# A two-layer transformer on one core: second-layer q and k projected between the layer norms, with changes to the first loads, a bias product and the tail of the first attention

## Chip, core and metric

The kernel runs on one core of a Trainium2 chip. The metric is the device time of one execution, in microseconds (us). The engines are TensorE (PE, with its weight loads PEld), VectorE (DVE), ScalarE (ACT), GpSimd (POOL) and SyncE (SP), which here only issues DMAs. All data are 32-bit floats. A 128x128 matmul against 512 columns appears in the trace as two records.

## What is computed

Two sequences (B = 2) of T = 2048 tokens with D = 256 features, 16 heads of 16. Each layer is an attention and a gated part that both read the normalized input; the layer's input x gets their product added.

```python
# layer 0, xn = layernorm(x)
attn = softmax(q @ k.T / sqrt(D)) @ v; attn = attn @ w_o.T + b_o + xn
Q, K = xn @ W_Q.T, xn @ W_K.T
out = branch(Q, K, V_fwd, W_fwd, U_fwd) + alpha * branch(Q @ W_inv.T, K @ W_inv.T, ...)
#   branch: (Q.V) * cumsum(K.W) per expert, weighted by softmax of a gelu router, times U, plus weights @ b
x = x + attn * silu(out @ W_O.T)
# layer 1, xn = layernorm(x)
attn = softmax(q @ k.T * HD**-0.5 + band mask of +-64) @ v; attn = attn @ w_out + b_out
gate = softmax(xn @ gate_w.T)                     # 8 experts
y = xn @ weight.T + sum_e gate_e/16 * (xn @ lora_U_e.T) @ lora_V_e.T
x = x + attn * silu(y)
```

## The kernel before

Features lie on partitions (two chunks of 128, NC = 2), tokens on columns. x, xn (normalized input) and gt (the gate) of both sequences stay in SBUF. Tokens go in blocks of 512 (TB; four blocks n per sequence). A scheduler orders the instructions of each engine ahead of time by their dependences and its own costs; what is marked keep_in_program_order ("pin") stays where the program puts it. Each engine works its list in order, and a wait holds everything behind it.

The stages, with lines:

- Start (L173 to L232). Weights of layer 0 come on ACT's and SP's DMA queues; load_x brings the eight x blocks. product (L204) multiplies weights together ahead of time; layer_norms (L95) runs the first layer's norms between these steps. A norm of one block is `there` (eight 128x128 transposes to tokens on partitions, xt, L104), statistics on DVE (L108, L110), Sqrt on ACT (L113), two small DVE steps, `back` (four scalings on ACT, xc, L121; eight transposes to xb, L127; copies to xn by ACT and DVE, L129).
- Layer 0's gate (L263 to L413): router (L277, L290), then for each block eight chunks of px, py, po (L387, L391, L371). The weights times b is the product of a 16-row bO with a 16-row wT, once for each output half (L403). we and wT come by SP from DRAM.
- attention(A0) (from L416). Projections of q and k (keys_queries, L456) go through DRAM (qd<-sb, L461) so that each head gets 32 rows; values (L469). Then a loop over steps s: 32 items (sequence b, head group g, block n) of U = 16 key tiles each. A step computes the transposed scores sk of item i and, U + 3 steps ahead, the untransposed sq for the row maxima (both L605), exponentials on ACT (L621), the maxima on DVE (L617), and one step later the weighted sum acc (L664). ACT copies acc to SBUF (`more`, L674) and POOL adds it to av (L675). After an item, its division is done by a chain of DMAs on SP (away, compact, invert, write, spread, divide), for the last item by PE and DVE (last_there L725 to L729, last_back L742). project (L750) multiplies by the output weights, DVE multiplies by gt (L755), POOL adds to x (L756). sk, acc, pr and others share one PSUM ring of four banks, tag "m".
- In the last U + 3 = 19 steps there is no sq any more.
- Layer 1's norms (L905 to L923): as before, for all eight blocks, with the router gates (L849), their return to tokens on partitions (tokens, L860), softmax (normalized) and turned (L876), which sends the weights through DRAM to 16 rows per expert (ge).
- Experts (L883): per block pt, po (L887, L893), tg on DVE, a second matmul with lV (L897), Silu, update of x with the attention bias times the gate.
- attention(A1), with the band: keys_queries for sequence 0 (16 jobs, L456), values for sequence 0, then sequence 1's projections while the first scores run.

Weights of an attention live in one pool, wat0 for layer 0, closed after its attention, then wat1.

Of the kernel before, what the change touches and what calls it, by code (L numbers as in the profile page):

```python
# [10 lines left out]
F32 = mybir.dt.float32  # L11
I32 = mybir.dt.int32
AF = mybir.ActivationFunctionType
ALU = mybir.AluOpType
# [23 lines left out]
def two_layers(ctx: ExitStack, tc: tile.TileContext, a, out):  # L38
# [20 lines left out]
    load_x(0, 0)  # L59
# [13 lines left out]
    def load_attn(pool, l, eng):  # L73
        return dict(
            q=load(pool, f"wq{l}", [P, NC, D], rows(a[f"wq{l}"]), eng),
            k=load(pool, f"wk{l}", [P, NC, D], rows(a[f"wk{l}"]), eng),
            v=load(pool, f"wv{l}", [P, NC, D], rows(a[f"wv{l}"]), eng),
            o=load(pool, f"wo{l}", [P, NC, D], rows(a[f"wo{l}"]), eng),
            bq=load(pool, f"bq{l}", [P, NC], a[f"bq{l}"], eng),
            bk=load(pool, f"bk{l}", [P, NC], a[f"bk{l}"], eng),  # L80
            bo=load(pool, f"bo{l}", [P, NC], a[f"bo{l}"], eng),
            bv=load(pool, f"bv{l}", [P, NC], a[f"bv{l}"], eng),
        )
# [10 lines left out]

    def layer_norms(blocks, tmp, ps, between=lambda r: None):  # L95


        QT = TB // P

        def there(b, n):  # L100
            xt = ps.tile([P, QT, D], F32, name="xt", tag="xt")
            for t in range(QT):
                for c in range(NC):
                    nc.tensor.transpose(xt[:, t, bass.ts(c, P)], x[b][:, c, bass.ds(n * TB + t * P, P)], ident)  # L104
            st = tmp.tile([P, QT, 6], F32, name="st", tag="st")
            mv = tmp.tile([P, QT, 2], F32, name="mv", tag="mv")
# [4 lines left out]

            f = tmp.tile([P, 2, QT], F32, name="f", tag="f")
            nc.scalar.activation(f[:, 0, :], mv[:, :, 1], AF.Sqrt, bias=eps_t)  # L113
            nc.vector.reciprocal(f[:, 0, :], f[:, 0, :])
            nc.vector.scalar_tensor_tensor(f[:, 1, :], mv[:, :, 0], -1.0, f[:, 0, :], ALU.mult, ALU.mult)
# [16 lines left out]
        for r in range(len(blocks) + 1):  # L132
            first = there(*blocks[r]) if r < len(blocks) else None
            if held:
                back(*held)
            held = first
            between(r)
# [12 lines left out]
    layer0 = ctx.enter_context(ExitStack())  # L150
    wat0 = layer0.enter_context(tc.tile_pool(name="wat0", bufs=1))

# [6 lines left out]
    with tc.tile_pool(name="fw", bufs=1) as fw:  # L159
# [4 lines left out]
        bO = fw.tile([2 * KE, D], F32, name="bO")  # L164
# [4 lines left out]
        with tc.tile_pool(name="raw", bufs=1) as raw, tc.tile_pool(name="tn", bufs=2) as tn, tc.tile_pool(  # L169
# [3 lines left out]
            wq = load(raw, "wq", [P, NC, D], rows(a["W_Q"]), nc.scalar)  # L173
            wiT = load(raw, "wiT", [P, NC, D], rows(a["W_invT"]), nc.scalar)
            wk = load(raw, "wk", [P, NC, D], rows(a["W_K"]), nc.scalar)
# [14 lines left out]
            bT = load(raw, "bT", [P, NC, 2 * KE], rows(a["bT"]), nc.sync)  # L190
# [32 lines left out]
            product(lambda m: bO, bT, 2 * KE, woT)  # L223
# [10 lines left out]
        A0 = load_attn(wat0, 0, nc.sync)  # L234
# [13 lines left out]
        nc.vector.reciprocal(rn, rn)  # L248
        ones = fw.tile([P, TB], F32, name="ones")
# [13 lines left out]
        with tc.tile_pool(name="pa", bufs=2, space=PSUM) as pa, tc.tile_pool(  # L263
# [87 lines left out]
            with tc.tile_pool(name="ta", bufs=2) as ta:  # L351
                for b in range(B):
                    prev = None
                    for n in range(NB):
# [9 lines left out]
                        wT = ta.tile([2 * KE, TB], F32, name="wT", tag="wT")  # L364
                        nc.sync.dma_start(out=wT, in_=wd[b][:, cols])
# [36 lines left out]
                        for oc in range(NC):  # L402
                            nc.tensor.matmul(po[oc], bO[:, bass.ts(oc, P)], wT, start=False, stop=True)  # L403
# [12 lines left out]
    def attention(A, scale, local, final):  # L416
# [14 lines left out]
        with ExitStack() as st:  # L431
# [20 lines left out]
            def keys_queries(b, n, i, hf, bank, place):  # L452
                w, bias = ((A["k"], A["bk"]), (A["q"], A["bq"]))[i]
                ps = bank()
                for c in range(NC):
                    nc.tensor.matmul(  # L456
# [547 lines left out]
```

## Time and profile before

| | us |
|---|---|
| median of three runs | 2598.02 (2597.92 to 2598.47) |
| the profiled execution | 2595.75, span 2594.0 |
| PE busy | 2543.6 (98% of the span) |
| DVE, ACT, POOL busy | 1681.6, 1633.7, 893.3 |
| first PE matmul | at 8.21 |
| layer 0's gate, per block | 43.3 |
| attention 0's steps with sq, each | 2.93 |
| last scores of attention 0 end | about 2117.0 |
| layer 1's norms | 2132.7 to 2178.4 |
| experts | 2178.4 to 2236.5 |
| q and k of sequence 0, layer 1 | 2236.5 to 2264.2 |
| values of sequence 0, layer 1 | 2264.2 to 2279.7 |

The page gives busy time, and a busy engine need not be the one that sets the end: the chain of waits, followed back from the last instruction, tells which one does. The table's later rows come from the timeline of PE. Stretches (windows) give the busy time of each engine between two times. A time in brackets behind an instruction is how long its engine stood idle ahead of it, and whose signal ended that.

### The profile page before, as it was taken

The numbers are of one execution on the slowest core, as the hardware profiler recorded it, in microseconds if no ns is written. First come the engines' busy times: TensorE is split into PE (matmuls) and PEld (weight loads), VectorE is DVE, ScalarE is ACT, GpSimd is POOL, SyncE is SP. The second block draws the span as 40 slices with busy tenths as digits, with TensorE's granted clock in tenths as the row PEclk, the third lists the DMA queues.
The fourth block names the chain that finished last, engine by engine and source line by source line (L and its number), as shares of the span: only waits on it lengthen the run. The fifth ranks groups of instructions, "written<-read, shape, count | busy, mean of one in ns | idle before, by whom it ended". The sixth has DMA issues, their size and how long they took to land.

```text
span 2594.0 us, 48140 instructions
## 1 busy us (share of the span) xinstructions
PE 2543.6 (98%) x18916; PEld 1075.1 (41%) x18916; DVE 1681.6 (65%) x2755; ACT 1633.7 (63%) x3188; POOL 893.3 (34%) x836
## 2 busy tenths in 40 slices
PE   8999999999999999999999999999999988999998
PEld 5444444543333333333333333333333325467765
DVE  4143333258888888888777888888888714138875
ACT  5400000127888888888878888888888874236654
POOL 0000000102444444444444444444444440107776
PEclk9999999999999999999999999999999999999999
DMA  7031111320001001010000001010000012234542
GB/s 246 37 85 49 50 49 33 121 74 3 16 10 49 12 11 47 12 44 16 10 22 36 12 21 37 12 46 14 10 16 12 10 34 35 73 123 129 157 143 85
DMA packets 80098, 129.83 MB, mean 50 GB/s; under 512 B 27456, under 2 KB 32448, under 8 KB 77056
## 3 DMA queue, kind: packets, MB, share of 16 engines
q1 hardware_dynamic: 77824, 125.19, 15.4%
q8 instruction: 148, 2.42, 0.4%
q10 hardware_dynamic: 2048, 1.58, 0.2%
q14 instruction: 78, 0.64, 0.1%
HBM read 80.23 MB, written 45.97 MB: 49 GB/s over the span
## 4 chain that ended last, share of the span: by engine, by line
PE 93%; DVE 3%; DMA 2%; ACT 1%; issue 1%; POOL 0%; POOLq 0%; ACTq 0%; SPq 0%; DVEq 0%
PE sk L605 24%; PE acc L664 21%; PE sq L605 18%; PE pp L456 4%; PE py L391 4%; PE po L371 4%; PE px L387 4%; PE pr L750 2%; PE ph L277 2%; PE pp L469 2%; PE psf L204 1%; DVE seen L612 1%; PE po L893 1%; DMA q<-row 1%; PE xb L127 1%
## 5 line engine op out<-in xcount | busy, mean ns | idle before, releaser
L617 DVE TENSOR_REDUCE part<-sq 128x2 f32<-128x1024 f32 x1024 | 1206.6, 1221 | 302.2 <-PE sq L605 301.8
L621 ACT ACTIVATE e<-sk 128x512 f32<-128x512 f32 x2048 | 1063.0, 615 | 215.9 <-PE sq L605 194.2
L605 PE MATMUL sk<-q,k 32*128 32x512 f32 (+2 forms) x5632 | 1153.9, 533 | 12.3 <-DMA q<-row 5.5
L605 PE MATMUL sq<-k,q 32*128 32x512 f32 (+2 forms) x5120 | 1131.4, 569 | 1.3 <-DVE part L617 1.3
L675 POOL TENSOR_TENSOR av<-av,more 128x512 f32<-128x512 f32 x480 | 607.9, 1266 | 962.5 <-ACT more L674 962.4
L605 PEld LDWEIGHTS sk<-q,k 32*128 32x128 f32 x5632 | 530.3, 184 | 604.3 <-ACT e L621 491.8
L664 PE MATMUL acc<-e,v 128*32 128x512 f32 x4096 | 550.6, 605 | 0.0
L605 PEld LDWEIGHTS sq<-k,q 32*128 32x128 f32 x5120 | 403.5, 183 | 22.2 <-DVE part L617 12.2
L674 ACT COPY more<-acc 128x512 f32<-128x512 f32 x480 | 287.8, 600 | 2.5 <-PE acc L664 1.5
L664 PEld LDWEIGHTS acc<-e,v 128*32 128x32 f32 x4096 | 82.5, 108 | 391.5 <-ACT e L621 386.2
L407 ACT ACTIVATE gt<-po 128x512 f32<-128x512 f32 x16 | 9.5, 596 | 324.6 <-PE po L403 324.6
L612 DVE CUSTOM_DVE_ANT_0 seen<-sq,mask 128x256 f32<-128x256 f32 (+1 forms) x512 | 176.7, 408 | 48.7 <-PE sq L605 42.6
L413 POOL TENSOR_TENSOR x<-x,up 128x512 f32<-128x512 f32 x16 | 20.2, 1265 | 459.2 <-DVE up L410 459.2
L626 POOL TENSOR_SCALAR_AFFINE_SELECT xn<-xn 128x512 f32<-128x512 f32 x172 | 110.0, 671 | 90.7 <-ACT xn L621 89.6
L395 DVE TENSOR_TENSOR xs<-we,px 128x512 f32<-128x512 f32 x64 | 43.9, 685 | 136.5 <-PE px L387 135.4
L621 ACT ACTIVATE xn<-sk 128x512 f32<-128x512 f32 x172 | 90.7, 601 | 55.5 <-PE sk L605 26.9
L387 PE MATMUL px<-xn,FV 128*128 128x512 f32 x256 | 121.2, 595 | 0.0
L391 PE MATMUL py<-cum,FW 128*128 128x512 f32 x256 | 120.5, 593 | 0.6 <-DVE cum L360 0.6
L371 PE MATMUL po<-pr,UO 128*128 128x512 f32 x256 | 119.0, 592 | 0.0
L397 DVE TENSOR_TENSOR pr<-xs,py 128x512 f32<-128x512 f32 x64 | 44.0, 687 | 61.3 <-PE py L391 61.1
L755 DVE TENSOR_TENSOR upd<-gt,pr 128x512 f32<-128x512 f32 x32 | 22.0, 687 | 81.4 <-PE pr L750 76.3
L371 PEld LDWEIGHTS po<-pr,UO 128*128 128x128 f32 x256 | 48.6, 190 | 61.2 <-issue 60.5
(167 smaller groups left out, 1634.6 us busy)
## 6 DMA issues: line engine op xcount, KB each, us to landing
we<-wd SPq DMA_DIRECT2D x128, 128.0 KB
ad<-av SPq DMA_DIRECT2D x60, 256.0 KB
qd<-sb SPq DMA_DIRECT2D x48, 256.0 KB
k<-qd SPq DMA_DIRECT2D x10, 1024.0 KB
q<-qd SPq DMA_DIRECT2D x10, 1024.0 KB
xn<-ad SPq DMA_DIRECT2D x60, 128.0 KB
recb<-rd SPq DMA_DIRECT2D x60, 128.0 KB
q<-qd SPq DMA_DIRECT2D x12, 512.0 KB
```

What stands on the lines that cost most here:

```text
L371: nc.tensor.matmul(po[oc], UO[:, ch, bass.ts(oc, P)], pr, start=(ch == 0), stop=False)
L387: nc.tensor.matmul(px, FV[:, c, bass.ts(ch, P)], xn[b][:, c, cols], start=(c == 0), stop=(c == NC - 1))
L391: nc.tensor.matmul(py, FW[:, c, bass.ts(ch, P)], cum[:, c, :], start=(c == 0), stop=(c == NC - 1))
L456: nc.tensor.matmul(ps, w[:, c, bass.ts(hf, P)], xn[b][:, c, bass.ts(n, TB)], start=(c == 0), stop=(c == NC - 1))
L605: nc.tensor.matmul(o, lhs, rhs, start=True, stop=True)
L612: nc.vector.tensor_tensor_reduce(seen[:, lo:hi], sq[:, d, t * 2 * P + lo : t * 2 * P + hi], mask[:, lo:hi], 1.0, LOWEST, ALU.add, ALU.max, ...
L617: nc.vector.tensor_reduce(pt[:, pair[0] : pair[1] + 1, t, kb], sq, AX.X, ALU.max)
L621: nc.scalar.activation(e, t, AF.Exp, scale=scale)
L626: nc.gpsimd.affine_select(out=e[:, :, c, :], in_=e[:, :, c, :], compare_op=ALU.is_ge, fill=0.0, base=0, pattern=[[0, 4], [sign, P]], chann ...
L664: nc.tensor.matmul(acc[hp[j], o : o + hi - lo], vs[b][:, kt, vcols(g, j)], es[j][:, lo:hi], start=(r == 0), stop=(r == len(parts) - 1), sk ...
L674: nc.scalar.copy(more, acc)
L675: nc.gpsimd.tensor_tensor(avs[i], avs[i], more, ALU.add)
```

## The change

Seven edits together.

1. The first DMA on SP is wq of layer 0's gate, the first on ACT is its wiT; x(0,0) follows wq on SP.
2. bO and wT are held twice, at rows 0 to 15 and 32 to 47; the second output half takes the upper copy. bT gets 48 columns, wT a second DMA.
3. Both layers' attention weights share one set of buffers (pool wat). wq, wk, and lU with lV (in wv's buffer) of the second layer are loaded at step 0 of attention 0; its biases, gateT and baseT at the start; wo after attention 0; wv after the experts.
4. In the last 19 steps of attention 0 DVE adds acc straight from PSUM to av.
5. In those steps sequence 0's norm begins: its transposes in halves (norm_there), a copy to xn as a resting place and the statistics by DVE; one `factors` for all four blocks at the end. The scalings (norm_apply: two tiles of four on DVE, two on ACT), the transposes back, and gates, tokens and normalized of sequence 0 follow among the last item's division and projection.
6. Sequence 1's norm runs after the attention, and between its steps 12 of the 16 q and k projections of sequence 0; the other four come between the experts of the two sequences. attention(A1) starts with values(0). Their sb ring has three buffers.
7. In experts lV's product comes at once after its own po; ge comes by four DMAs per sequence with the rows in the order of rank, then expert (lU and lV are laid out to match), in place of eight. One PSUM pool serves this stage, with one pt bank and not two. The row buffer of attention 0's maxima is single.

```diff
-    load_x(0, 0)
...
-            wq = load(raw, "wq", [P, NC, D], rows(a["W_Q"]), nc.scalar)
+            wq = load(raw, "wq", [P, NC, D], rows(a["W_Q"]), nc.sync)
             wiT = load(raw, "wiT", [P, NC, D], rows(a["W_invT"]), nc.scalar)
+            load_x(0, 0)
...
-        bO = fw.tile([2 * KE, D], F32, name="bO")
+        bO = fw.tile([HP + 2 * KE, D], F32, name="bO")
+        twice = [slice(r * HP, r * HP + 2 * KE) for r in range(NC)]
...
-                        for oc in range(NC):
-                            nc.tensor.matmul(po[oc], bO[:, bass.ts(oc, P)], wT, start=False, stop=True)
+                        for oc, r in enumerate(twice):
+                            nc.tensor.matmul(po[oc], bO[r, bass.ts(oc, P)], wT[r, :], start=False, stop=True)
...
+    def norm_there(b, n, half, bank, tmp, mv, copy, issue=lambda i: i):
+        H2 = QT // 2
+        xt = bank().rearrange("p (t d) -> p t d", d=D)
...
+        rest = resting(b, n, half)
+        copy(rest, xt)
...
+            nc.vector.bn_stats(st[:, t, :], rest[:, t, :])
+    def norm_apply(b, n, f):
+        for t in range(QT):
+            rest = resting(b, n, t // 2)[:, t % 2, :]
+            if t % 2:
+                nc.scalar.activation(rest, rest, AF.Identity, scale=f[:, 0, t : t + 1], bias=f[:, 1, t : t + 1])
+            else:
+                nc.vector.tensor_scalar(rest, rest, f[:, 0, t : t + 1], f[:, 1, t : t + 1], ALU.mult, ALU.add)
...
+                elif i * U + u >= len(items) * U - U - LEAD and u:
+                    nc.vector.tensor_tensor(avs[i], avs[i], acc, ALU.add)
...
+                for r in range(2 * NB):
+                    n, half = divmod(r, 2)
+                    at(total - U - LEAD + 1 + 2 * r, norm_there, 0, n, half, single, op, mv[:, tile_of(n), :], nc.vector.tensor_copy, pin)
+                at(total - 1, factors, nf, mv, pin)
+                for f, *args in (
+                    (last_there, last),
+                    (norm_apply, 0, 0, nf[:, :, tile_of(0)]),
+                    (last_back, last),
+                    (back, 0),
+                    (norm_apply, 0, 1, nf[:, :, tile_of(1)]),
+                    (project, last, 0),
...
+            there(0)
+            project(2)
+            there(1)
+            factors(nf[:, :, two(0)], mv[:, two(0), :])
+            whole_bias(A1, small())
+            turned(pl, 0)
+            project(2)
+            norm_apply(1, 0, nf[:, :, tile_of(0)])
+            norm_apply(1, 1, nf[:, :, tile_of(1)])
+            there(2)
+            project(1)
+            there(3)
+            factors(nf[:, :, two(1)], mv[:, two(1), :])
+            project(1)
+            norm_back(1, 0, bank)
...
+            project(len(jobs))
+            for n in range(NB):
+                experts(1, n)()
+    A1["v"] = weight(1, "v")
+
+    attention(A1, float(HD ** -0.5), True, True, projected=True)
```

Here project(count) is count of keys_queries for sequence 0 of layer 1.

## The prediction

> **What bounds the kernel now.** I read the page's busy shares and its chain first, then the stages by time, then the groups of instructions and their waits inside the stages that the diff touches. From the page:
>
> ```profile
> PE 2543.6 (98%) x18916; PEld 1075.1 (41%) x18916; DVE 1681.6 (65%) x2755; ACT 1633.7 (63%) x3188; POOL 893.3 (34%) x836
> PE 93%; DVE 3%; DMA 2%; ACT 1%; issue 1%; POOL 0%; POOLq 0%; ACTq 0%; SPq 0%; DVEq 0%
> ```
>
> 93% of the chain is TensorE (PE). Such a kernel is shortened by removing PE work from the chain, or by filling the places where PE waits. The stages between the two attentions show where that is: attention 0's last steps, its drain, the layer norms, the experts, the q/k projection of sequence 0.
>
> ```profile
> 2067.60:2117.00 49.40, 49.40 (x314) 12.79 (x317) 3.43 (x7) 45.13 (x93) 27.70 (x22) 1.00 0.04 12
> 2117.00:2132.70 15.70, 10.85 (x41) 4.39 (x37) 3.04 (x6) 4.95 (x8) 6.42 (x6) 0.89 0.13 36
> 2132.70:2178.40 45.70, 34.84 (x288) 23.31 (x288) 25.18 (x112) 27.92 (x56) 1.27 (x1) 0.85 0.09 25
> 2178.40:2236.50 58.10, 57.15 (x144) 25.39 (x144) 17.89 (x29) 12.93 (x22) 0.46 (x1) 1.00 0.27 38
> 2236.50:2264.20 27.70, 27.67 (x65) 12.09 (x65) 0.75 (x1) 10.30 (x15) 9.42 (x10) 1.00 0.42 126
> ```
>
> Columns: stretch, its length, then busy time of PE, PEld, DVE, ACT, POOL. In rows 2 and 3 (61.4 us) PE stands still for 15.7 us, and what it does is short transposes; the chain of waits there gives 33 us to PE and 30 to DVE, ACT and hand-overs. Row 5 is pure PE, full, needing only block data that exist 60 us earlier. So row 5 can fill rows 2 and 3. Single waits, from PE's timeline:
>
> ```profile
> 8.21 3.75 PE L204 MATMUL psf<-wq,wiT 128*128 128x256 f32 x8 [8.21 <-DMA wiT<-in_W_invT]
> ...
> 258.47 1.98 PE L403 MATMUL po<-wT,bO 16*128 16x512 f32 x4
> 260.38 1.98 PE L387 MATMUL px<-xn,FV 128*128 128x512 f32 x4
> ...
> 2115.80 1.14 PE L605 MATMUL sk<-q,k 32*128 32x512 f32 x8
> ...
> 2123.42 0.66 PE L725 MATMUL tr<-ident,av 128*128 128x128 f32 x4 [2.57 <-POOL av L675]
> ...
> 2138.15 2.70 PE L127 MATMUL xb<-ident,xc 128*128 128x128 f32 x8 [3.50 <-ACT xc L121]
> ```
>
> PE's first matmul waits 8.2 us for a weight. The two bias matmuls of a block (L403) take 260.38 − 258.47 = 1.91 us one after the other, while four score matmuls (L605) with 32 rows each take 1.07 us start to end in the chain.
>
> **What the Trainium skill says.** "TensorEngine Tiling (Array Packing)", Key Properties: row tiles of 32 work in parallel when they lie in different row groups. L605 agrees: four of 512 columns in 1.07 us, where one full-array matmul of 512 columns takes 0.86 (two of L456 in 1.72). "DMA: Bandwidth & Descriptors", Queues, rings and completion order: the engines take turns between queues packet by packet. The first load agrees: below. Same page, Anatomy of one DMA: about 2.0 us fixed plus bytes over 436 GB/s; the chain of waits agrees on the fixed part, with 2.69 us for 8 KB (rd<-dn) and 2.37 for 128 KB (recb<-rd). "TensorE: Matmul & The Clock Gate", Part 1: after idling the array runs at half rate until it has been busy some 3.4 us. L204's first 16 records take 0.47 us each, its last 32 take 0.22.
>
> **The change part by part**, against the profiled execution (2595.75 us, span 2594.0), which is 2.27 below the median 2598.02.
>
> 1. *First transfers.* wq leads SP's queue, wiT leads ACT's, x(0,0) goes behind wq. Now wiT is second on ACT, while SP moves x. Data flow from 2.4 us at 370 GB/s; x rows have 2 KB, weight rows 1 KB, so ACT's queue has a third, 123 GB/s: 0.52 MB in 4.2 us, 6.6 us, and PE starts 1.5 later. After: the two weights come first, 0.52 MB at 370 GB/s is 1.4 us, so 3.8 + 1.5 = 5.3. Gain 2.9, I take 2.7. Next are wk and x(0,0), some 2 us of data later, by 7.5; they are needed at 9.7 and 13.3. No other load is waited for in the first 60 us. Bounds 1.0 and 4.7 (the clock may also rise during the second product). SP gets seven more small loads (some 3 us); its next urgent transfer, wd, is issued at 117 us, the queue is through by 64.
> 2. *Bias pair.* The second copy of bO and wT lies 32 rows higher, so both matmuls run in two row groups: 1.91 becomes 0.86 + 0.15. 8 blocks × 0.9 = 7.3 us, all on PE, which is busy 43.0 of 43.0 us per block there. It costs one more wT DMA per block, 0.31 us on SP, which idles in that stage. The price of a pair is not shown; bounds: 1.91 (nothing gained) and 0.86 (8.4).
> 3. *Attention 0's last 19 steps.* ACT's copies (0.49 of 2.45 us a step) and POOL's adds go; DVE adds from PSUM (0.69), it was idle. ACT then needs 4 × 0.49 = 1.96 a step, PE 2.07. Added on PE: sequence 0's transposes, 32 × 0.11 = 3.5. New PE sum: 19 × 2.07 + 3.5 + 0.2 (pmx) + 4 × 1.91 (L750) = 50.7, now 52.2. DVE gets per two steps 2 × 0.69 + 0.69 + 0.9 = 3.0 of 4.6. The PSUM ring "m" of four now serves the transposes too; each bank is read one step later, so I expect no wait. Gain 1.0; bounds +1.5 and −3.
> 4. *Drain and sequence 0's norms.* After the last scores: L750 1.9, acc 1.0, add 0.75, tr 0.7, DVE's reciprocal and division 1.0, of 1.5, back-transposes 4 × 0.87, L750 2 × 1.72, gates 4 × 0.72, tokens 0.8: 17.4. Evacuations I set at 1.5, the PSUM pools' change 0.7: 19.6.
> 5. *Sequence 1's norms with q and k.* PE: there 3.5, back 3.5, gates 2.9, tokens 0.8, turned 1.8, bias 1.0, twelve projections × 1.72 = 20.6: 34.1, plus 1.0 of waits. The chain norm_there, copy, statistics, factors, apply takes some 6 us twice; between the two ends stand 5 to 6 us of projection. ACT has 25 us of work in it. Each projection brings its SP transfer (256 KB); ge needs 4 broadcasts instead of 8.
> 6. *Experts.* 8 × 6.87 + turned 1.8 + four projections 6.9 = 63.7; the one pt bank is free after 0.7 us, behind 3.4 us of po.
> 7. *A new wait.* The layer's wv shares its buffer with lU and lV, so its load starts after the last expert matmul, and values(0), next on PE, needs it: 0.5 issue + 2.4 + 0.6 data = 3.5. v's memset (4.1 us of 8.26 for two, POOL) now also starts there, but six PSUM banks cover the last us. Behind values(0) on PE stand sequence 1's projections and the first scores, all moved by the wait. On SP the q/k fetches queue behind wv; PE needs them 20 us later. Bounds of the wait: 2.5 and 6.
>
> The other moved loads cost nothing: wq, wk, lU, lV of the second layer are issued on SP at attention 0's step 0, when PE has read the old buffers, and behind them stands q<-row of a block 13 steps (38 us) away; wo follows the last L750, and its first reader, the bias product, comes some 10 us later; gateT and baseT leave ACT's queue, where their issue took 0.4 to 0.5 us each between the last exponentials.
>
> Sum of 4 to 7: 19.6 + 35.1 + 63.7 + 3.5 = 121.9 against rows 2 to 5, 147.2: gain 25.3. All parts: 2.7 + 7.3 + 1.0 + 25.3 = 36.3. 2595.75 − 36.3 = 2559.5; with the 2.27, **2562**. The main loops issue the same instructions in the same order, at no cost.
>
> **The rivals.**
> - *In-order ACT holds PE in part 5.* Applies, copies, sb and gT stand in one queue behind waits on DVE. About twelve hand-overs from DVE, each holding PE 0.8 us, take 10 back: 2572. For it: the norms now have PE waits of 3.5 us; against: q/k stand between.
> - *The pair stays serial.* Both write full columns; then 7.3 is lost: 2569. Against: L605 overlaps in the same form.
> - *Better.* The half clock of the norm stage (0.85 granted) goes, and the start warms earlier: another 7, 2555.
> - *Slower: the ring of three sb.* A projection waits until the DMA of the third before has landed, and ACT, holding, keeps norms and PE waiting. With landing time L, twelve jobs take 4 × (L + 0.7); it eats 36 us from 4(L + 0.7) = 71, L = 17 us. At L = 20 the time is 2609. Against: before, sixteen such jobs ran at 1.72 us each on a ring of four without one wait, so L is below 6.2.
> - *Nothing changes:* only if parts 4 to 7 give back all; no view supports that.
>
> **How the numbers follow.** Likeliest case 0.53 (2555 to 2569), ACT 0.20, pair 0.10, better 0.10, none 0.02, slower 0.05. The range, 2551 to 2576, takes the first four with their bounds and leaves the upper tail of the ACT case out. A measurement here tells some 0.2%, 5 us, from no change. Faster 0.93, same 0.02, slower 0.05.
>
> **What would show it.** PE's first matmul near 5.3 us; the bias group's start-to-next at 1.0 us; steps of 2.1 to 2.5 us before the drain; values starting some 36 us earlier than 2264.2, after one PE wait of 3 to 4 us for wv; no PE wait over 1.5 us between. PE waits for ACT above 8 us in the norms mean the first rival; waits of ACT for qd<-sb mean the slower one.

## The result, and the profile after

| | before | after |
|---|---|---|
| median of the runs | 2597.97 us (2595.76 to 2598.47) | 2564.17 us (2561.18 to 2568.23) |
| profiled execution | 2595.75, span 2594.0 | 2565.4, span 2563.7 |
| after / before | | 0.9873, 95% interval 0.9855 to 0.989 |

The change saves 33.8 us by the medians and 30.3 us between the two profiled spans. I had said 2562 (36.3 us less). The runs after scatter by 7 us, those before by 2.7 here; beside the later experiments the kernel before scattered by 3.0 to 12.5 us, so a wide scatter is not a mark of the change. What can differ between two executions of one kernel is the main thing that the experiments found.

The page's busy line and its chain, after. The chain's listed shares add up to 81% only, so I used it for the order of engines and not for sums: PE leads DVE by far, as before, and is now busy for 99% of the span.

```profile
PE 2528.7 (99%) x18916; PEld 1071.3 (42%) x18916; DVE 1701.7 (66%) x2788; ACT 1621.6 (63%) x3157; POOL 875.2 (34%) x818
PE 77%; DVE 2%; DMA 1%; issue 1%; ACT 0%; POOLq 0%; POOL 0%; SPq 0%; DVEq 0%; ACTq 0%
```

The stretches after, cut where the work changes: the last 19 steps of attention 0; the drain with sequence 0's norms; sequence 1's norms with the projections; the experts with the other projections; the wait for wv and values(0). Columns as in the prediction: stretch, length, busy time of PE, PEld, DVE, ACT, POOL, granted clock of PE.

```profile
2060.90:2110.50 49.60, 49.60 (x345) 15.17 (x341) 27.02 (x63) 38.73 (x76) 7.76 (x7) 1.00 0.04 12
2110.50:2132.00 21.50, 17.89 (x144) 10.12 (x140) 11.30 (x29) 10.74 (x19) 4.98 (x4) 0.92 0.05 14
2132.00:2165.10 33.10, 33.07 (x188) 18.83 (x189) 19.27 (x61) 22.50 (x40) 10.64 (x8) 1.00 0.40 116
2165.10:2229.50 64.40, 64.40 (x179) 28.47 (x177) 18.10 (x31) 17.34 (x27) 0.00 (x0) 1.00 0.14 41
2229.50:2251.30 21.80, 18.48 (x69) 14.08 (x68) 8.73 (x19) 0.60 (x1) 0.41 (x4) 0.84 0.51 205
```

Row 3 is what the change was about: before, PE was busy for 34.84 of 45.70 us of the norm stage; now sequence 1's norms hold PE busy for 33.07 of 33.10. What idle time is left lies in row 2 (3.6 us) and row 5 (3.3 us), and both rows have a granted clock under 1. The same five places in PE's timeline as before:

```profile
5.03 3.78 PE L251 MATMUL psf<-wq,wiT 128*128 128x256 f32 x8 [5.03 <-DMA wiT<-in_W_invT]
...
256.49 1.13 PE L457 MATMUL po<-wT,bO 16*128 16x512 f32 x4
257.55 1.98 PE L440 MATMUL px<-xn,FV 128*128 128x512 f32 x4
...
2115.86 0.66 PE L788 MATMUL tr<-ident,av 128*128 128x128 f32 x4 [1.36 <-DVE av L732]
2118.34 1.06 PE L805 MATMUL of<-ident,over 128*64 128x128 f32 x8 [1.83 <-DVE over L792]
...
2232.55 18.27 PE L530 MATMUL pp<-wv,xn 128*64 128x256 f32 x68 [2.85 <-DMA wv<-in_wv]
```

The first matmul starts 3.2 us earlier. The bias pair takes 257.55 − 256.49 = 1.06 us, where it took 1.91. In the drain PE waits for the last sum (1.36) and for the division (1.83). Values(0) start at 2232.55 instead of 2264.2, after the new wait for wv, 2.85 us of idle time; but they then take 18.3 us, and before they took 15.5.

Reading the same landmarks in both traces gives where the 30.3 us came from:

| from, to | before | after | gain | predicted |
|---|---|---|---|---|
| start to the first bias pair | 171.08 | 171.13 | −0.05 | 2.7 |
| to attention 0's first projection (eight pairs) | 306.59 | 299.93 | 6.66 | 7.3 |
| to the end of the last scores | 1639.27 | 1639.53 | −0.26 | 1.0 |
| to the start of values(0) | 147.25 | 121.96 | 25.29 | 25.3 |
| to the first scores of attention 1 | 23.06 | 25.85 | −2.79 | 0 |
| to the end | 306.75 | 305.30 | 1.45 | 0 |
| sum | 2594.0 | 2563.7 | 30.30 | 36.3 |

The large term was right to 0.1 us, as a sum. Two things eat 5.5 us in this trace: the start's gain is gone by the first bias pair, and values(0) run slowly behind the wait for wv. The tail of the first attention, third row, gained nothing. The last row's 1.45 us is no effect that I can name: in later traces of the same kernel and its variants this stretch took 304.9 to 307.2.

### The profile page after: what moved, and what is told of

Read it like the earlier page. It is cut to its first block, busy times and chain, and to the rows that moved or that the text cites. A ratio compares the mean times of both kernels' runs of the same rounds, so it can differ in the third digit from the quotient of the medians.

```text
span 2563.7 us, 48097 instructions
## 1 busy us (share of the span) xinstructions
PE 2528.7 (99%) x18916; PEld 1071.3 (42%) x18916; DVE 1701.7 (66%) x2788; ACT 1621.6 (63%) x3157; POOL 875.2 (34%) x818
## 4 chain that ended last, share of the span: by engine, by line
PE 77%; DVE 2%; DMA 1%; issue 1%; ACT 0%; POOLq 0%; POOL 0%; SPq 0%; DVEq 0%; ACTq 0%
PE sk L665 24%; PE acc L724 22%; PE sq L665 18%; PE pp L477 4%; PE pr L813 2%; PE pp L530 2%; PE po L1002 1%; DVE seen L672 1%; DVE xn L780 1%; PE pt L998 1%; PE po L1010 1%; DMA q<-row 0%; PE pmx L702 0%; PE xb L138 0%; PE xb L113 0%
## 5 line engine op out<-in xcount | busy, mean ns | idle before, releaser
L738 POOL TENSOR_TENSOR av<-av,more 128x512 f32<-128x512 f32 x462 | 586.0, 1268 | 940.1 <-ACT more L737 940.1
L737 ACT COPY more<-acc 128x512 f32<-128x512 f32 x462 | 270.9, 586 | 1.0 <-issue 0.5
L444 PEld LDWEIGHTS py<-cum,FW 128*128 128x128 f32 x256 | 48.4, 190 | 61.5 <-issue 59.8
```

Source lines behind the costliest of these rows:

```text
L444: nc.tensor.matmul(py, FW[:, c, bass.ts(ch, P)], cum[:, c, :], start=(c == 0), stop=(c == NC - 1))
L737: nc.scalar.copy(more, acc)
L738: nc.gpsimd.tensor_tensor(avs[i], avs[i], more, ALU.add)
```

## The experiments

Each median stands beside the kernel before on the same chip; "saved" is the difference of the two. The intervals of the ratios are about 0.0015 to each side, some 4 us, so differences of 1 or 2 us between variants are read from traces and not from this table.

| run | median us | saved us | ratio to before, 95% interval |
|---|---|---|---|
| again | 2563.22 | 31.8 | 0.9883, 0.9867 to 0.9898 |
| serial_pair | 2570.61 | 24.4 | 0.9904, 0.9891 to 0.9918 |
| old_first | 2564.11 | 30.9 | 0.9881, 0.9866 to 0.9897 |
| own_wv | 2559.01 | 36.0 | 0.986, 0.9846 to 0.9873 |
| bare_norms | 2570.54 | 27.1 | 0.9898, 0.9883 to 0.9913 |
| cover_wv | 2560.65 | 37.0 | 0.9856, 0.984 to 0.9873 |
| old_tail_add | 2566.02 | 31.6 | 0.9883, 0.9868 to 0.9897 |
| warm_start | 2559.75 | 37.9 | 0.9861, 0.9846 to 0.9876 |
| best | 2559.41 | 35.2 | 0.9867, 0.9854 to 0.988 |
| bare_pinned | 2577.99 | 16.6 | 0.9939, 0.9926 to 0.9953 |
| before_pair | 2588.55 | 6.0 | 0.9977, 0.997 to 0.9983 |
| own_warm | 2557.34 | 39.4 | 0.9846, 0.9832 to 0.9859 |

**The changed kernel again (no edit).**

> The changed kernel as it is, once more, as the common yardstick of the runs beside it. Both theories: 31 to 34 us under the kernel before.

It saved 31.8 us. Its profiled execution, span 2558.8, is 4.9 us shorter than the first one of the same kernel, and this turned out to be the most useful pair of traces. PE's timeline of the first two products, in the first execution:

```profile
5.03 3.78 PE L251 MATMUL psf<-wq,wiT 128*128 128x256 f32 x8 [5.03 <-DMA wiT<-in_W_invT]
9.33 3.78 PE L251 MATMUL psf<-wk,wiT 128*128 128x256 f32 x8 [0.52 <-DVE aq L256]
```

and in the second:

```profile
4.69 3.78 PE L251 MATMUL psf<-wq,wiT 128*128 128x256 f32 x8 [4.69 <-DMA wiT<-in_W_invT]
8.99 1.99 PE L251 MATMUL psf<-wk,wiT 128*128 128x256 f32 x8 [0.52 <-DVE aq L256]
```

The same eight records take 3.78 us in one and 1.99 in the other: in the first PE is still at half rate. The first bias pair stands at 171.13 and 167.39. The second execution also has its wait for wv, and there values(0) do not slow down (22.8 us from their start to attention 1's first scores; 25.85 in the first execution). So 3.7 us at the start and 3.1 us behind the wait are matters of one execution and not of the program. (The spans differ by less than these two together, because the second execution took 0.6 us more from the last scores to values(0) and 1.3 more in the last stretch.)

**Both bias matmuls in one row group.**

```diff
-  po[oc], bO[r, bass.ts(oc, P)], wT[r, :], start=False, stop=True
+  po[oc], bO[twice[0], bass.ts(oc, P)], wT[twice[0], :], start=False, stop=True
```

> The changed kernel, with both bias matmuls of a block taking the lower copies of bO and wT, so that they share one row group; the order of PE's instructions is the same. Theory (two row groups overlap): the start-to-next goes from 1.05 back to 1.9 us, 8 blocks x 0.87 = 7.0 us slower than the changed kernel, that is some 24 to 26 us under the kernel before. Rival (the overlap is eaten by a wait further on, or the gain lay in the changed order of the first block): under 3 us slower.

```profile
258.43 1.98 PE L457 MATMUL po<-wT,bO 16*128 16x512 f32 x4
260.34 1.98 PE L440 MATMUL px<-xn,FV 128*128 128x512 f32 x4
```

The pair takes 1.91 us again (PE's timeline of serial_pair), and the kernel is 7.4 us slower than `again` on the same chip; 7.0 was expected. From the first bias pair to the eighth, the trace has 303.60 us here, 297.64 in `again`: 0.85 us for each pair. The overlap of two row groups is what pays.

**The old order of the first transfers.**

```diff
-  wq = load(..., nc.sync);   wiT = load(..., nc.scalar);  load_x(0, 0)
+  load_x(0, 0);  wq = load(..., nc.scalar);  wiT = load(..., nc.scalar)
```

> The changed kernel with the first transfers as before: x(0,0) ahead on SP, wq and wiT on ACT. Theory (the earlier start is lost again, because PE idles for 1.5 us at 18 us and then runs at a slow clock, and because later waits absorb the rest): the first matmul at 8.2 us, but the total within 1.5 us of the changed kernel. Rival (the gain stands as predicted, the loss seen in one trace was chance): 2.7 us slower than the changed kernel.

It was 0.9 us slower than `again` by the medians, which speaks for the theory, but the intervals don't tell 0.9 from 2.7, so the traces must. Here the first matmul starts at 8.52 and the first bias pair at 172.68. The changed kernel and those of its variants that start like it and keep its order of instructions here have that pair at 167.39, 167.40, 168.66, 168.88, 171.01, 171.13, 171.30 and 171.36. So the earlier transfers are worth 1.3 to 5.3 us at that place, against the one trace of old_first. The eight traces' records of the granted clock tell them apart. Full clock first stands at 8.0 to 9.0 us in the first four and at 13.4 to 14.0 in the other four; and in all but the first two a stretch of 3.41 us at half clock comes between 18 and 25 us, after PE's wait of 1.5 us for ACT. My theory was therefore half right: the wait and the slow clock are there in six of eight traces, and in the four slowest 1.3 to 1.7 us are left of a first matmul that starts some 3.5 us earlier. The gain is not lost altogether.

**A buffer of its own for wv.**

```diff
     lU, lV = lUV
+    late = ctx.enter_context(tc.tile_pool(name="late", bufs=1))
+    A1["v"] = load(late, "wv1", [P, NC, D], rows(a["wv1"]), nc.sync)
...
-    A1["v"] = weight(1, "v")
```

> The changed kernel with a buffer of its own for the second layer's wv, loaded when the first attention ends, so that values(0) needs not wait for it. Theory (the wait of 2.9 us makes the clock fall, and the first matmuls behind it take double for 3 us more): 5.5 to 6 us faster than the changed kernel, values(0) in 15.5 us. Rival 1 (only the wait itself is lost): 3 us faster. Rival 2 (v's memset on POOL comes last once wv is there): no gain, values(0) waits for POOL.

```profile
2226.61 15.23 PE L530 MATMUL pp<-wv,xn 128*64 128x256 f32 x68 [0.69 <-ACT gt L1016]
```

In PE's timeline the wait for wv is gone; 0.69 us for ACT stands in its place (a PSUM bank still read by the last Silu), and values(0) take 15.2 us. From the last scores to attention 1's first scores it takes 142.5 us; 147.8 and 145.3 in the two executions of the changed kernel. By the medians it is 4.2 us faster than `again`. Values(0) start 119.7 us after the last scores, as against 122.0 and 122.6: 2.2 to 2.8 us are lost by the wait every time, the slow clock behind it comes only sometimes. Each of the first two theories was half right. POOL's memset was not waited for here; in the changed kernel it runs much earlier, during sequence 1's norms (2136.8 to 2145.1 us in the first trace).

**Projections in place of the wait.**

```diff
-            project(len(jobs))
             for n in range(NB):
                 experts(1, n)()
+            project(len(jobs))
```

> The changed kernel with its four leftover projections behind the last expert block instead of between the two sequences' experts, so that PE has 6.9 us of work while wv loads. Theory (only the load holds PE): the wait of 2.9 us is gone and no slow clock follows, as in the run with a buffer of its own: 3 to 5 us faster than the changed kernel. Rival (the q and k transfers of these four now queue with wv and delay the fetches that the first scores wait for): no gain.

It saved 37.0 us. From the last scores to attention 1's first scores: 142.7 us, as with the buffer. No memory is needed for it: the four leftover projections were simply put where nothing hid the load.

**The wait and the clock, over all traces.** Eight traces of the changed kernel and its variants have the wait for wv (2.7 to 3.0 us). From the start of values(0) to attention 1's first scores they took 22.77, 22.77, 22.78, 22.78, 24.36, 24.41, 24.46 and 25.85 us. The four without it took 22.80, 22.80, 22.80 and 22.81. So in half of the executions the wait costs 1.6 to 3.1 us more than itself. The Trainium skill, "TensorE: Matmul & The Clock Gate", Part 1, says that the window over which PE's activity is judged runs freely and doesn't begin with the kernel, so the same program meets it at different places. The traces' records of the granted clock agree: the stretches at half clock last 3.41 us or twice that, and in the first trace of the changed kernel they begin at 20.20, 2119.40 and 2232.04 us, whole multiples of 3.413 us apart. Behind the wait for wv that trace has two such stretches, the three traces of about 24.4 us have one, the other four none. The same page also says that the clock falls after at least one idle window of about 3.4 us; here an idle time of 2.85 us was enough, and the measurement decides.

A much shorter wait was followed by half clock, too. PE's timelines of own_wv and bare_norms, which have the same program at this place, where attention 0's first projections wait 1.17 us for ACT:

```profile
467.33 3.70 PE L477 MATMUL pp<-xn,wk 128*128 128x512 f32 x8 [1.17 <-ACT gt L461]
```

```profile
468.59 5.40 PE L477 MATMUL pp<-xn,wk 128*128 128x512 f32 x8 [1.17 <-ACT gt L461]
```

In bare_norms the granted clock is half from 468.79 to 472.20 us. Six of the fourteen traces have such a stretch behind this wait (serial_pair, bare_norms, bare_pinned and the three runs with matmuls of zeros, below); it costs 1.7 us, and from attention 0's first projection to the end of the last scores these six take some 1.7 to 2.1 us longer than the changed kernel, whatever their edit.

**Norms without projections.**

```diff
 # sequence 1's norm steps
             there(0)
-            project(2)
             there(1)
...                                  # all nine project(1) and project(2) go
             project(len(jobs))       # now sixteen
```

> The changed kernel with none of sequence 0's q and k projections between sequence 1's norm steps: all sixteen come between the experts of the two sequences. Theory (the norms leave PE idle, and the twelve projections fill that): before, half of the norm stage took 22.9 us, now it takes 33.3 with 20.6 us of projections in it, so the bare norms take some 22 us and the projections 20.6 more: 9 to 10 us slower than the changed kernel. Rival (what saved the time is the other order of the norm steps itself, halves through one copy, and not the projections): under 3 us slower.

It fell between the two: 4.7 us less saved than by `again`, and from the last scores to values(0) 126.9 us, as against 122.0 and 122.6 in the two executions of the changed kernel. PE's timeline of bare_norms shows what I had not thought of:

```profile
2132.86 1.10 PE L998 MATMUL pt<-xn,lUV 128*128 128x512 f32 x2
2133.80 0.60 PE L113 MATMUL xb<-ident,x 128*128 128x128 f32 x4
2134.23 1.02 PE L998 MATMUL pt<-xn,lUV 128*128 128x512 f32 x2
2135.09 1.02 PE L1002 MATMUL po<-xn,baseT 128*128 128x512 f32 x2
2135.95 0.60 PE L113 MATMUL xb<-ident,x 128*128 128x128 f32 x4
```

L998 and L1002 are sequence 0's expert matmuls. Sequence 0's norm is done by then, so the scheduler drew them between sequence 1's transposes (L113). They fill most of the norms, up to one wait of 2.96 us for tg on DVE. DVE was not idle ahead of tg: one scaling of the norm (L132), 0.50 us long at most other places, took 3.23 us there (more on it below). So a second experiment had to keep the expert matmuls out.

**Norms with nothing between.**

```diff
 # as bare_norms, and pt, po of experts and the gates of sequence 1 are pinned:
-  nc.tensor.matmul(pt, lU[:, c, :], ...)
+  tc.keep_in_program_order(nc.tensor.matmul(pt, lU[:, c, :], ...))
```

> As bare_norms (no projections between sequence 1's norm steps), and sequence 0's expert matmuls are held in program order behind the last gates of sequence 1, so that the scheduler can't fill the norms with them as it did in bare_norms. Theory (norms alone leave PE idle some 9 to 10 us; in bare_norms the experts filled half of it): from the last scores to values(0) 131 to 133 us as against 122 in the changed kernel and 127 in bare_norms; 9 to 11 us slower than the changed kernel, half-rate clock after the waits included. Rival (bare_norms lost its time elsewhere, to the wait of 2.96 us for tg and the clock behind it, and bare norms cost little): no longer than bare_norms.

PE's four largest waits in the norm stage, 2131.4 to 2160 (us in total, times, longest):

```profile
PE xb L138 <- DVE xn L132: 3.6, 1, 3.6
PE pw L985 <- ACT gT L987: 1.5, 1, 1.5
PE xb L113 <- ACT xn L119: 1.1, 1, 1.1
PE s L939 <- DVE lg L949: 0.9, 1, 0.9
```

From the last scores to values(0) it takes 136.0 us, 14 us more than the changed kernel (I had expected 131 to 133), and the kernel saves 16.6 us instead of 31.8. In this stretch PE is idle for 16.7 us, 6.5 in the changed kernel, and the clock is half for 10.2 us, 3.9 in the changed kernel. Two parts of the idle time are not the fault of bare norms alone. The pins also keep other matmuls from between the transposes that send sequence 1's weights (L985) in the experts, where PE waits three times for ACT, 2.1 us in all. And the longest wait, 3.55 us, is for one DVE scaling that took 3.86 us, not 0.50.

That scaling stands in all twelve traces of the changed kernel and its variants: one of them takes 2.87 to 3.86 us, starts while POOL runs the second memset of v (L513, 4.2 us), and ends 0.14 or 0.15 us after it. The reason is not shown, and no run keeps the memset out of the norms. The changed kernel has projections on PE at that time and does not wait.

So filling sequence 1's norms is worth 14 us in this comparison, and at least some 8.5 without these two parts (an estimate: 14.0 less 2.1 and at most 3.4). By bare_norms, 9 of the 14 us also come from other work of sequence 0. What the change needs is one sequence ahead of the other, and independent matmuls; those of another kind did a large part of it, not all.

**The add in the tail as before.**

```diff
-  elif i * U + u >= len(items) * U - U - LEAD and u:
-      nc.vector.tensor_tensor(avs[i], avs[i], acc, ALU.add)
```

> The changed kernel with acc copied by ACT and added by POOL in the last 19 steps too, as before, instead of the single add on DVE; sequence 0's norm steps stay there. Theory (ACT with five passes of 0.49 us a step would again set the pace, and the transposes come on top): the 19 steps take 51 to 53 us instead of 49.6, and the drain waits some 1 us longer for the last sum: 2.5 to 4.5 us slower than the changed kernel. Rival (PE sets the pace in both, the add is hidden either way): within 1 us of it.

```profile
2117.85 0.66 PE L785 MATMUL tr<-ident,av 128*128 128x128 f32 x4 [2.57 <-POOL av L735]
```

The 19 steps (from the last sq to the end of the last scores) take 51.21 us; 50.62 with DVE's add, 50.35 before. The transposes back of the last sum (tr) start 6.48 us after the last scores instead of 5.27. That makes 0.6 and 1.2 us, 1.8 in all, less than the 2.5 that the theory asked for. By the start of values(0) 0.9 to 1.5 us of it are left (from the first bias pair 2062.94 us here, 2061.42 and 2062.01 in the two executions of the changed kernel); the medians (31.6 us saved, `again` 31.8, the first measurement 33.8) can't tell it from nothing. So neither theory nor rival fits in full: the old add is not hidden, and it costs less than I thought.

**PE kept busy while the first weights come.**

```diff
+            zero = raw.tile([P, D], F32, name="zero");  nc.vector.memset(zero, 0.0)
+            idle = ps_f.tile([P, TB], F32, name="psf", tag="psf")
+            for _ in range(4):
+                tc.keep_in_program_order(nc.tensor.matmul(idle[:, :D], zero[:, :P], zero, start=True, stop=True))
```

> The changed kernel with four matmuls of 128x256 zeros on PE ahead of the first product, while the first weights are on their way; nothing reads their result. Theory (PE's clock is low after idling, and it is chance whether the second product still runs at half rate: two traces of the same start had 3.78 us for it, two had 1.99): the first product takes 2 to 2.5 us instead of 3.78 and the second 1.99 every time; the first router matmul starts at 52 us or earlier, as against 57.1 and 53.4 in the two traces of the changed kernel: 1 to 4 us faster than it. Rival (the start is bound by the loads of x and the weights and not by PE's rate): no change after 60 us.

```profile
1.39 3.78 PE L243 MATMUL psf<-zero 128*128 128x256 f32 x8 [1.39 <-DVE zero L240]
4.97 2.45 PE L257 MATMUL psf<-wq,wiT 128*128 128x256 f32 x8
7.93 1.56 PE L257 MATMUL psf<-wk,wiT 128*128 128x256 f32 x6 [0.52 <-DVE aq L262]
```

In PE's timeline of warm_start the cold 3.8 us now fall on zeros; the first real product is through in 2.45 us and the second runs at full rate. The first bias pair starts at 165.88 (166.10 and 166.77 in the two later runs that have this edit), as against 167.4 to 171.4. The scheduler also orders the first 100 us in another way, so its router matmuls at 44.6 are not compared with others, and what the order and what the clock gave is not told apart. It saved 37.9 us, 4 to 6 more than the changed kernel in its two measurements. But all three traces with this edit have the half clock behind the 1.17 us wait ahead of attention 0's first projections, and lose there 1.7 us or more of what the start had gained; at the end of the last scores warm_start stands at 2107.46 us, `again` at 2106.84, the first trace of the changed kernel at 2110.59. Three traces are too few to say whether the edit brings that about.

**All three, with the division first.**

```diff
 # own_wv and warm_start, and in the drain DVE's order is pinned
-  nc.vector.reciprocal(rec, ps[:, :, :, HD])
+  pin(nc.vector.reciprocal(rec, ps[:, :, :, HD]))
...
-  (norm_apply, 0, 0, nf[:, :, tile_of(0)]),
+  (norm_apply, 0, 0, nf[:, :, tile_of(0)], pin),
```

> The changed kernel with three edits: a buffer of its own for wv of the second layer, the four matmuls of zeros ahead of the first product, and DVE's order in the drain fixed so that the last item's division comes ahead of sequence 0's scalings. Theory (the wait for wv, the slow clock at the start, and three scalings of 0.52 us ahead of the division each cost PE its time): 2.5 to 3 us from the wait, 1.5 to 5 at the start, and some 1 us in the drain (PE's wait for the division 1.83 to 0.8 us or less, its start 7.75 us after the last scores brought to 6.7 or earlier): 5 to 9 us faster than the changed kernel, 2555 to 2559 us. Rival (the scalings put later only move the wait to the transposes back; the start's gain is lost in later waits): 3 us faster, by wv alone.

DVE's timeline of the changed kernel in the drain shows why I tried this: between the last sum (L732) and the division (L792) stand four scalings (L132) of sequence 0's norm, 0.5 us each.

```profile
2115.12 0.68 DVE L732 TENSOR_TENSOR av<-av,acc 128x512 f32<-128x512 f32 x1
2115.72 1.55 DVE L132 TENSOR_SCALAR xn<-xn,nf 128x256 f32<-128x256 f32 x3
2117.19 0.24 DVE L791 RECIPROCAL dn<-tr 128x16 f32<-128x16 f32 x1
2117.36 0.32 DVE L132 TENSOR_SCALAR xn<-xn,nf 128x256 f32<-128x256 f32 x1
2117.60 0.60 DVE L792 TENSOR_TENSOR over<-tr,dn 128x256 f32<-128x256 f32 x1
```

With the division first, PE's wait for it falls from 1.83 to 1.09 us and `of` starts 7.01 instead of 7.75 us after the last scores. But the scalings of blocks 2 and 3 are now late, and PE's timeline of best has two new waits:

```profile
2123.96 0.52 PE L138 MATMUL xb<-ident,xn 128*128 128x128 f32 x3 [0.69 <-DVE xn L132]
...
2125.13 0.77 PE L138 MATMUL xb<-ident,xn 128*128 128x128 f32 x5 [0.66 <-DVE xn L132]
```

From the last scores to values(0): 120.6 us, 119.7 in own_wv. The rival was right on this edit: 0.74 us gained, 1.35 given back in these two. The kernel as a whole saved 35.2 us, not more than own_wv or warm_start alone by this measurement.

**The buffer and the zeros, without the division.** The edits of own_wv and warm_start together.

> The changed kernel with two of the last version's three edits: wv of the second layer in a buffer of its own, and the four matmuls of zeros ahead of the first product; DVE's order in the drain is left as in the changed kernel. Theory (the division put first only moved PE's wait to the transposes back and cost 0.8 us): from the last scores to values(0) 119.7 us as in the run with the buffer alone, as against 120.6 in the last version; start as in it, so 0.5 to 1 us faster than the last version in the trace, and 4 to 7 us faster than the changed kernel. Rival (the 120.6 came from elsewhere): 120.6 again.

From the last scores to values(0) 119.7 us, as the theory said; the trace's span is 2556.5, against 2557.2 of the last one. By its median it is 5.6 us further from the kernel before than the first measurement of the changed kernel, 7.5 further than `again`, and the lowest ratio of all. But the intervals of own_wv, cover_wv and warm_start overlap with its own, and the trace of own_wv alone is shorter, 2555.4 us: without the half clock at 467 us it reaches the end of the last scores at 2106.87, own_warm at 2108.30. So that the two gains add up is not shown.

**The bias pair alone, on the kernel before.** The edits of bO, bT, wT and the two matmuls, as in the change.

> The kernel before with the bias pair alone: bO and wT held twice, 32 rows apart. Theory (a pair takes 1.05 us instead of 1.91, 8 times, less 1.3 us that the other order of the first block costs, where transposes of the router's weights are put ahead of px and wait for ACT): the last bias pair starts 6.0 us after its place relative to the first, the total 5 to 6 us faster than the kernel before. Rival (the gain seen in the changed kernel needed the other edits): under 3 us faster.

6.0 us, as expected, 0.9977 with an interval of 0.997 to 0.9983. In its trace the first pair stands at 172.55 (171.08 before) and the pairs after it gain 0.90 us each (297.63 instead of 303.92 us over seven). So 1.5 us are lost ahead of the first pair. Of these 0.3 are there already at 134 us (a py matmul starts at 134.44, 134.13 before); the other 1.2 come a little later, at a place that can be read in PE's timeline of the changed kernel,

```profile
138.08 0.49 PE L379 MATMUL pw<-ident,lg 128*16 128x128 f32 x3 [0.67 <-ACT wo L381]
138.41 1.02 PE L440 MATMUL px<-xn,FV 128*128 128x512 f32 x2
```

where three transposes of sequence 1's router weights (`turned`), and a wait of 0.67 us for ACT, stand ahead of px. In the kernel before, px comes first. The scheduler orders these anew because of the pair's second wT transfer or the wider bO; which of the two was not tried.

## Why the prediction was right, and where its steps were off

- **Part 1, first transfers, 2.7 us: the mechanism was right, the size lies inside a spread that I had only as bounds.** The first matmul came at 5.03 (5.3 predicted), 4.69 to 5.03 over the traces. The gain is 1.3 to 5.3 us at the first bias pair, about the bounds of 1.0 and 4.7; I had put into the bounds that the clock may rise by the second product, and it did in four of eight traces of this start. The half clock between 18 and 25 us, in six of eight, I had not. The row −0.05 of the table is this gain (1.4 to 1.6 in that trace) less what is lost ahead of the first pair, part 2.
- **Part 2, bias pair, 7.3 us: right, with one term missing.** 1.06 us a pair (1.0 predicted), 0.85 to 0.90 saved by each, 7.4 us by serial_pair. What failed is "the main loops issue the same instructions in the same order, at no cost": the first block's order changed, and that costs 1.2 us. Another 0.5 us goes where the last pair is followed by attention 0's first projection, whose wait for ACT's Silu grew from 0.7 to 1.2 us.
- **Part 3, the last 19 steps, 1.0 us: no gain; the 50.7 came near by chance, and the 52.2 has no source.** Measured alike, the stretches are 50.62 after and 50.35 before. The 52.2 stands in no view, and how it was reached is not shown; steps of 2.45 us, which I took for the pace, are 13 of 19 in the trace, the earlier ones take 2.07 to 2.27 without projections. In the sum of 50.7 two errors cancel: the stretch holds three projections of L750, not four (the fourth is counted again in part 4), 1.9 too many; and the eight halves of transposes lengthen their steps by 0.45 to 0.70 us each, 5.2 in all and not 3.5. Steps of 2.07 instead of 2.45 bring back 13 × 0.38 = 4.9, so the transposes were all but paid for by DVE's add.
- **Part 4, drain, 19.6 us: 21.4. The step that failed is the clock, which the sum has at full rate throughout.** PE's idle time was 3.6 us, and my terms for it (add, division, evacuations, pools) make 3.95. PE's busy time was 17.9 us, and my terms make 15.7: the clock was half from 2119.40 to 2122.81 us, so a projection takes 2.75 us there and the next one 1.88. A stretch of 3.41 us at half rate costs 1.7 us, an estimate from its length. That makes most of the 2.2 us of surplus work; all twelve traces of this kernel and its variants have one or two such stretches in the drain. The scheduler did put scalings ahead of the division, but that makes only 0.74 of the wait of 1.83 us, and the attempt to mend the order gained nothing.
- **Part 5, 35.1 us, and part 6, 63.7: 33.1 and 64.6,** with one us of sequence 1's gates drawn over into the experts; 97.7 for both instead of 98.8. PE's waits inside both add up to 0.3 us, so the rival of ACT in order is refuted; ACT itself waited for PE (4.8 us in all for pp). The slower rival, the ring of three sb, has no wait in the trace either. Of the better rival the full clock in the norms came (1.00 instead of 0.85), but parts 5 and 6 had priced their work at full rate already.
- **Part 7, wait for wv, 3.5 us: 2.85, but the price is larger than the wait.** I bounded the wait and did not ask what PE does after it, although my own reading of the start had shown half rate after idling. In half of the traces 1.6 to 3.1 us follow. This is the step that failed for the profiled execution; it is what own_wv and cover_wv take away. The formula for one DMA that the prediction took from the Trainium skill, "DMA: Bandwidth & Descriptors", Anatomy of one DMA, is given there for DMAs that GpSimd issues, and wv comes by SP; the 2.85 us are the measured price. And v's memset did not start here, as I had said, but in the norms.
- **The sum of parts 4 to 7** was right to 0.1 us (121.96 and 121.9) because the drain's 1.8 too many and the 1.8 too few of the other parts cancel: a coincidence of the parts, not a proof of each.
- **The statement of what would show it** held for the first matmul (5.03) and the bias pair (1.06). The wait for wv was 2.85 us and not 3 to 4. The steps ahead of the drain took 2.07 us or, with transposes, 2.65 to 2.77, so about half of them lie above the 2.5 that I had named. Values started 31.6 us earlier and not 36: 2.75 of the start, 0.64 of the pairs and 1.26 of the tail were missing. One PE wait over 1.5 us stood between, that for the division.

That the total came within 2.2 us of 2562 is partly luck: missed gains in the start, the tail and behind the wait met 1.45 us in the last stretch that I cannot name, and the runs of this kernel spread by 7 us.

That filling the norms is the main cause of the large term is shown by bare_pinned (14 us back, with the two reservations made there), and that other matmuls fill a large part too by bare_norms. The traces also say where the 25.3 us went: from the last scores to values(0) PE is idle for 16.7 us before and 6.5 after, and the clock is half for 17.1 us before (five stretches of 3.41) and 3.9 after, worth at most half of the difference, 6.6 us; some 5.2 us of sequence 0's transposes moved ahead into the last 19 steps, where faster steps paid for them. How the rest divides among the steps of the norms was not tried apart.

## What to carry to other kernels

Where one engine sets the time and a stage leaves it idle for hand-overs, let one half of the data run ahead, so that the stage has independent matmuls to draw from; a scheduler then finds fillers by itself, and an experiment that takes one filler out must keep the next one from slipping in. When a new wait on TensorE is priced, ask what the clock does behind it, and cover the wait with work that is needed anyway (here four projections that only had to change places). Carry one gain on to later landmarks before it is counted: 1.5 us and more won at the start were lost again 300 us later to a slow clock behind a wait of 1.2 us. And read landmarks from the same instructions in both traces before a stage is called faster: a number of before that stood in no view made a gain of 1.0 us here where there was a loss of 0.3.

## What the runs showed of the hardware that I had not expected

- Two executions of one kernel can differ by 5 us in span (2563.7 and 2558.8) with the same instructions and the same waits: 3.7 us at the start, where the second product took 3.78 or 1.99 us, and 3.1 us behind the wait for wv, less 1.9 at other places. The page's mean clock gives it only in the third digit (0.997 and 0.999).
- The clock's half-rate stretches come in lengths of 3.41 us on a fixed grid (20.20, 2119.40 and 2232.04 us in one trace). Idle times of PE well under that length were followed by one: 2.85 us ahead of values(0) in four of eight traces, 1.2 us or less ahead of attention 0's first projections in six of fourteen.
- In all eight traces of the new start, the first matmul began between 4.69 and 5.03 us. The four that began at 4.80 or earlier had full clock at 8.0 to 9.0 us, the four from 4.81 on only at 13.4 to 14.0. I have no test of whether the order by start is more than chance.
- Four matmuls of zeros that nothing reads, 3.8 us of them, did not delay the first product (4.97 us) and took the first slow phase onto themselves. A gain of the whole kernel by them is not shown.
- Two matmuls of 16 rows and 512 columns, in two row groups, took 1.06 us from the start of the pair to the next instruction, 1.91 in one row group.
- A DVE scaling of 128x256, mostly 0.50 us long, took 2.87 to 3.86 us where a memset of 128x4879 ran on POOL beside it, and ended 0.15 us after the memset, in all twelve traces. DVE's statistics beside the first of the two memsets took 0.41 us as elsewhere. The cause was not tested.
